# Last sublayer of a four-layer decoder: fp32 rows split into two float32r halves, and the last normalising moved to ScalarE

## Chip, cores and metric

The kernel runs on one core of a Trainium2 chip, as one launch. The metric is the device time of that launch in microseconds (us): before the change the median of three runs is 4253.46 us (4248.44 to 4256.29). "PE" is the matmul engine (TensorE), "PEld" its weight loads, "DVE" is VectorE, "ACT" ScalarE, "POOL" GpSimd, and "SP" the engine whose queue issues the DMAs.

## Reference, cut to the last sublayer

A decoder of four layers (self-attention, cross-attention and a feed-forward part each, with a different form in every layer) runs over 64 x 64 tokens of 256 channels. Every sublayer ends in `x = layernorm(x + sublayer(x))`. The change touches the last sublayer alone, a feed-forward part with ternary weights ("bitlinear"):

```python
def absmax_quant(x):
    gamma = max(abs(x), axis=-1, keepdims=True)
    x_hat = clip(x * 128 / gamma, -128 + EPS, 128 - EPS)
    return x_hat * gamma / 128                  # clipped, not rounded
def ternarize_weights(w):
    gamma = mean(abs(w))
    return sign(round(w / (gamma + EPS))) * gamma
def bitlinear(x, w):
    return einsum('bsd,od->bso', absmax_quant(layer_norm(x)), ternarize_weights(w))
h = gelu(bitlinear(x, w_fc), approximate=False) # w_fc: 1024 x 256
x = layernorm(x + bitlinear(h, w_proj))         # w_proj: 256 x 1024
```

All of it is fp32. The weights are -1, 0 or 1 times one number, and that number is applied after the product.

## The kernel before

**Tiles.** The 4096 tokens are 8 groups (`g`) of 4 tiles (`t`) of 128 tokens, 32 tiles in all. The rows `X[g]` stay in SBUF for the whole kernel, as do the eight buffers `CT[g]` (128 x 1024 fp32), which hold the transposed context until the cross-attention of layer 3 has read its group. After that the last sublayer uses `CT[g]` for the normalised and clipped rows of group `g` (`l3_prepare`).

**The last sublayer** (`l3_ffn`) walks over the 32 tiles with a pipeline that is written out for PE. In iteration `i`, PE has, in this order: the eight 128 x 128 transposes of tile `i-3` (`turned`, into two PSUM banks), the first product of tile `i` (`hidden`, 256 to 1024), in two of four tiles the transposes of the next group's rows (`turn`), and the second product of tile `i-3` (`output`, 1024 to 256). Around PE a tile needs, in this order:

- ACT: Gelu of the first product out of PSUM in two halves (L2402);
- DVE: statistics of the 1024 values in two halves (L339), joined (L342), variance plus epsilon (L311); POOL: the power -1/2 (L313); DVE: minus mean times that (`nmr`, L2337); ACT: the normalising, 128 x 1024 (`hn`, L2342);
- DVE: largest absolute value (`am`, L2348), two small steps (L2349, L2350), and the clipping in two passes over 128 x 1024 (L2353, L2354);
- PE: transposes (L319); ACT: two copies 128 x 512 out of PSUM (L2412); PE: the second product (L2419);
- DVE: scale and residual (`z`, L2421), statistics (L339, L342, L311); POOL: power (L313); DVE: the last normalising into `X` (L2423); SP: the DMA of the result.

While the first six groups run, `parts` adds a quarter of the same preparation (`l3_prepare`, L2334 to L2354) of the group two further on to each tile.

**Who sets the order.** PE's order is the program's (`manual_schedule` for PE). On DVE, ACT, POOL and SP a planner puts the instructions into an order when the program is built, with its own costs and times; on the chip every engine then takes its instructions strictly in that order, and each waits for the semaphores of what it reads.

**Weights.** `ternary` loads a weight (1 MB) into a buffer of the ring, DVE sums its absolute values over 128 x 2048 (L2315), POOL sums over the partitions (L2316), and then POOL (L2325) and DVE (L2326) replace the weight by -1, 0, 1 in four pieces, with `CT[3]` and `CT[4]` for scratch. The loads were issued at 3174.3 and 3199.4 us of the profiled execution, and the pieces made between 3520.8 and 3625 us, all inside the cross-attention before.

**fp32 on PE.** One `matmul` of fp32 operands in the program shows in the trace as two MATMUL records, each with a weight load of its own: the 4 products of `hidden` are 8 records, the 8 of `output` 16.

Of the kernel before, what the change touches and what calls it, by code (L numbers as in the profile page):

```python
# [9 lines left out]

F32 = mybir.dt.float32
BF16 = mybir.dt.bfloat16
# [19 lines left out]
class Linear:  # L32
# [68 lines left out]
    def first(self, pool, bank, fill):  # L101
# [41 lines left out]
class ContextRows:  # L143
# [3 lines left out]
    def __init__(self, dec):  # L147
# [12 lines left out]
    def fill(self, n, pool, tag, bufs, banks, copy):  # L160

        dec = self.dec
        while n and self.units:
# [12 lines left out]
class L1Ffn:  # L176
# [21 lines left out]
    def weights(self):  # L198
# [80 lines left out]
class Decoder:  # L279
# [2025 lines left out]
            late=late, ready=ready, key_turned=key_turned, turned=turned, scores=scores, output=output, values=values, end=end,  # L2305
        )

    def ternary(self, name):

        nc, ins = self.nc, self.ins  # L2310
        w = self.weight(name)
        n = ins[name].shape[1]
        self.load(w.rearrange("p (c n) -> p c n", n=n), ins[name].rearrange("(c p) n -> p c n", p=P))
        col, gam = self.small(1, "tcol", bufs=2), self.small(1, "tgam", bufs=2)
        nc.vector.tensor_reduce(col, w, AX.X, ALU.add, apply_absolute_value=True)  # L2315
        nc.gpsimd.partition_all_reduce(gam, col, P, bass_isa.ReduceOp.add)  # L2316
        nc.vector.tensor_scalar_mul(gam, gam, 1.0 / (P * WCOLS))

        thr = self.small(2, "tthr", bufs=2)
        nc.vector.tensor_scalar(thr[:, 0:1], gam, 1e-6, 0.5, ALU.add, ALU.mult)  # L2320
        nc.vector.tensor_scalar_mul(thr[:, 1:2], thr[:, 0:1], -1.0)
        for i in range(4):
            part = w[:, i * 512 : (i + 1) * 512]
            below = self.CT[3 + i // 2][:, i % 2, :]
            nc.gpsimd.tensor_scalar(below, part, thr[:, 1:2], None, ALU.is_lt)  # L2325
            nc.vector.scalar_tensor_tensor(part, part, thr[:, 0:1], below, ALU.is_gt, ALU.subtract)  # L2326
        return w.rearrange("p (c n) -> p c n", n=n), gam

    def l3_quantized(self, out, src, n):

# [42 lines left out]
    def l3_ffn(self, ctx):  # L2373

        nc = self.nc
        HID = 1024
        wfc, gfc = self.ternary("l3f_wfc")  # L2380
        wpr, gpr = self.ternary("l3f_wproj")
        AHEAD = 2
        wk = self.pool(ctx, "l3f", 2)
        groups, state = {}, {}

        def turn(g, c):
            if c == 0:
                groups[g] = wk.tile([P, 2, NTOK], F32, tag="xt", name="xt")
            ps = self.transpose4([self.l3_rows[g][:, t, c * P : (c + 1) * P] for t in range(TG)], "xt")
            nc.scalar.copy(groups[g][:, c, :], ps)  # L2390

        def hidden(g, t):
            xt = groups[g]
# [12 lines left out]
            return hn  # L2406

        def turned(h):
            ht = wk.tile([P, 8, P], F32, tag="ht", name="ht")
# [3 lines left out]
            return ht  # L2413

        def output(g, t, ht):
            x = self.X[g]
            ps = self.bank("o", tag="acc", bufs=2)
            for j in range(8):
                nc.tensor.matmul(ps[:, :D], ht[:, j, :], wpr[:, j, :], start=j == 0, stop=j == 7)  # L2419
            z = wk.tile([P, 1, D], F32, tag="z", name="z")  # L2420
            nc.vector.scalar_tensor_tensor(z[:, 0, :], ps[:, :D], gpr, x[:, t, :], ALU.mult, ALU.add)  # L2421
            mv, rstd = self.mean_rstd(z, 1, 1e-5)
            nc.vector.tensor_scalar(x[:, t, :], z[:, 0, :], mv[:, 0, 0:1], rstd, ALU.subtract, ALU.mult)  # L2423

        tiles = [(g, t) for g in range(self.n_groups) for t in range(TG)]
        n = len(tiles)
        with self.tc.manual_schedule(engines={mybir.EngineType.PE}):
            for g in range(len(self.l3_rows), AHEAD):
                for part in self.l3_prepare(g):
                    part()  # L2430
            groups[0] = self.l3_first
            parts, hts = [], {}
            for i in range(n + 3):

                for j in range(i - 3, i - 2 if i < n else min(i - 1, n)):
# [12 lines left out]
                if parts:  # L2448
                    parts.pop(0)()
# [93 lines left out]
```

## Time and profile before

| | |
|---|---|
| runs, median | 4253.46 us |
| span of the profiled execution | 4250.0 us |
| cross-attention of layer 3 ends (last product L2274) | 3963.8 us |
| last sublayer, from there to the end | 286 us |
| first products of the last sublayer, L2398 | 256 records of 128 x 512, 3963.4 to 4222 us |
| second products, L2419 | 512 records of 128 x 256 |
| Gelu, L2402 | 64 of 128 x 512, mean 689 ns |
| copies out of PSUM, L2412 | 64 of 128 x 512, mean 577 ns |
| last normalising, L2423 | 32 of 128 x 256 on DVE, mean 411 ns |
| power -1/2, L313 in the last sublayer | 65 of 128 x 1, mean 627 ns; 6 of 128 x 4, mean 1103 ns |

Busy time is the time in which an engine has an instruction in it; matmuls overlap one another, so the distance from one start to the next tells their cost better than the mean duration. The share of a whole span mixes stages with different limits; for the change only the last 286 us and the stage just before count.

### The profile page before, as it was taken

The page shows a single profiled execution, that of the slowest core. Times are in us where ns is not written, and L with a number is a line of the kernel's source. Part 1 is how long each engine was busy: PE and PEld are TensorE (multiplying, and loading weights), DVE is VectorE, ACT ScalarE, POOL GpSimd, SP SyncE. Part 2 cuts the span into 40 slices and gives each one's busy share as a digit, 9 for nine tenths or more (in the row PEclk, how much of TensorE's full clock was granted, in tenths as well). Part 3 has the DMA queues.
Part 4 walks back from the last instruction along what each step waited for, and adds up shares of the span by engine and source line. Part 5 has one row for each costly group of instructions (what it writes and reads, how often), then busy time and mean ns, then how long its engine had stood idle before and what let it go on. Part 6 is the DMA issues. An engine that isn't in the chain of part 4 may idle for free.

```text
span 4250.0 us, 74130 instructions
## 1 busy us (share of the span) xinstructions
PE 4051.5 (95%) x28788; PEld 2618.4 (62%) x28808; DVE 3042.7 (72%) x6107; ACT 2106.4 (50%) x3863; POOL 1506.3 (35%) x1553
## 2 busy tenths in 40 slices
PE   8889999989998999989999999999999999999998
PEld 5645556666675555546666666666656666666666
DVE  6844548888685688877777777777766777777786
ACT  5555635767634577544444444444433444444443
POOL 4511112242341111115555555555544444444111
PEclk9989999999999999999999999999999999999999
DMA  2200002333300000031111111111131100000000
GB/s 81 73 21 10 1 26 69 72 84 71 82 1 12 1 1 1 10 132 28 26 31 26 26 31 26 26 30 27 26 102 28 26 23 21 23 23 16 11 16 18
DMA packets 108294, 144.00 MB, mean 34 GB/s; under 512 B 15844, under 2 KB 73380, under 8 KB 106536
## 3 DMA queue, kind: packets, MB, share of 16 engines
q1 hardware_dynamic: 106984, 137.69, 12.7%
q8 instruction: 228, 3.74, 0.4%
q10 hardware_dynamic: 960, 1.57, 0.2%
q14 instruction: 122, 1.00, 0.1%
HBM read 70.25 MB, written 26.76 MB: 23 GB/s over the span
## 4 chain that ended last, share of the span: by engine, by line
PE 65%; DVE 15%; ACT 6%; POOL 4%; issue 3%; DMA 1%; SPq 0%; POOLq 0%; ACTq 0%; DVEq 0%
PE p L1777 19%; PE acc L2066 5%; PE acc L2274 4%; PE sq L1208 3%; PE ret L1247 2%; PE qT L319 2%; PE acc L1396 2%; POOL rstd L313 2%; DVE bnst L339 2%; PE gate L911 2%; DVE mc L1213 2%; PE gate L1592 2%; PE sk L1211 2%; PE s L2004 2%; PE up L911 2%
## 5 line engine op out<-in xcount | busy, mean ns | idle before, releaser
L313 POOL TENSOR_TENSOR rstd<-rstd,neg_half 128x1 f32<-128x1 f32 (+1 forms) x195 | 157.9, 810 | 653.1 <-DVE rstd L311 585.2
L313 POOL TENSOR_TENSOR hrq<-hrq,neg_half 128x4 f32<-128x4 f32 x256 | 258.7, 1011 | 300.7 <-DVE hrq L311 283.9
L1213 DVE TENSOR_REDUCE mc<-sq 128x2 f32<-128x512 f32 x512 | 317.1, 682 | 63.9 <-PE sk L1211 63.7
L1219 ACT ACTIVATE e<-sk 128x512 f32<-128x512 f32 x512 | 265.5, 608 | 112.1 <-PE sk L1211 111.5
L1208 PE MATMUL sq<-l1x 32*128 32x256 f32 x2048 | 275.2, 407 | 4.9 <-DVE z L1094 3.1
L1777 PE MATMUL p<-l3a_wq,xt 128*128 128x512 f32 x512 | 243.8, 599 | 11.2 <-DVE v L300 9.9
L313 POOL TENSOR_TENSOR hrk<-hrk,neg_half 128x4 f32<-128x4 f32 x160 | 188.2, 1176 | 185.8 <-DVE hrk L311 181.0
L1211 PE MATMUL sk<-l1x 32*128 32x256 f32 x2048 | 252.9, 392 | 0.0
L1777 PE MATMUL p<-l3a_wk,xt 128*128 128x512 f32 x512 | 247.1, 605 | 0.0
L1208 PEld LDWEIGHTS sq<-l1x 32*128 32x128 f32 x2048 | 208.3, 195 | 58.8 <-issue 23.6
L1777 PE MATMUL p<-l3x_wq,xt 128*128 128x512 f32 x512 | 242.3, 596 | 0.3 <-DVE k L2168 0.3
L1777 PE MATMUL p<-l3a_wv,xt 128*128 128x512 f32 x512 | 233.9, 599 | 0.4 <-ACT y L94 0.4
L2274 PE MATMUL acc<-l3x_wo,yt 128*128 128x256 f32 x1024 | 232.4, 380 | 1.6 <-DVE yt L300 1.0
L2066 PE MATMUL acc<-l3a_wproj,yt 128*128 128x256 f32 x1024 | 232.0, 379 | 0.5 <-DVE yt L300 0.5
L2066 PEld LDWEIGHTS acc<-l3a_wproj,yt 128*128 128x128 f32 x1024 | 194.2, 190 | 53.7 <-issue 29.2
L2274 PEld LDWEIGHTS acc<-l3x_wo,yt 128*128 128x128 f32 x1024 | 190.5, 190 | 33.9 <-issue 7.7
L1211 PEld LDWEIGHTS sk<-l1x 32*128 32x128 f32 x2048 | 188.5, 187 | 7.3 <-issue 2.9
L2237 POOL TENSOR_TENSOR s<-s,smx 128x512 f32<-128x512 f32 x64 | 66.9, 1046 | 333.8 <-DVE smx L2236 319.8
L319 PEld LDWEIGHTS qT<-ident,q 128*128 128x128 f32 x1024 | 121.9, 141 | 95.9 <-issue 75.2
L2050 POOL TENSOR_TENSOR hry<-hry,neg_half 128x8 f32<-128x8 f32 x64 | 106.2, 1659 | 183.4 <-DVE hry L2046 183.4
L319 PE MATMUL qT<-ident,q 128*128 128x128 f32 x1024 | 157.4, 277 | 3.3 <-ACT qT L2208 2.4
L1247 PE MATMUL ret<-e,vt 128*32 128x256 f32 x2048 | 140.6, 390 | 18.2 <-DVE mc L1213 17.2
(415 smaller groups left out, 10209.4 us busy)
## 6 DMA issues: line engine op xcount, KB each, us to landing
vs<-v SPq DMA_DIRECT2D x308, 128.0 KB
l3x_kv<-kv SPq DMA_DIRECT2D x28, 256.0 KB
x<-in_x SPq DMA_DIRECT2D x8, 512.0 KB
ct<-in_ctxT SPq DMA_DIRECT2D x8, 512.0 KB
cn<-in_ctx SPq DMA_DIRECT2D x8, 512.0 KB
l1x<-in_ctx SPq DMA_DIRECT2D x128, 32.0 KB
l1x_x<-x SPq DMA_DIRECT2D x8, 512.0 KB
l1x<-l1x_x SPq DMA_DIRECT2D x128, 32.0 KB
```

Of the source, the lines that this page charges most:

```text
L313: nc.gpsimd.tensor_tensor(out, out, self.neg_half[:, :n], ALU.pow)
L319: self.nc.tensor.transpose(ps[:, j * P : (j + 1) * P], blk, self.ident)
L911: nc.tensor.matmul(ps[:n], w[:, c, h0 : h0 + n], xt[:, c, :], start=c == 0, stop=c == 1)
L1208: nc.tensor.matmul(ps[:, n, :], x_[rows, j, part], c_[rows, j, :], start=True, stop=True)
L1211: nc.tensor.matmul(ps[:, n, :], c_[rows, j, part], x_[rows, j, :], start=True, stop=True)
L1213: nc.vector.tensor_reduce(mc[new % 2][:, ra + k, 2 * j : 2 * j + 2], ps, AX.X, ALU.max, negate=True)
L1219: nc.scalar.activation(es[rb + k], ps, AF.Exp, scale=scale)
L1247: nc.tensor.matmul(ret[32 * r : 32 * r + 32, :], vt[i % 2][:, lc, 4 * r + j, :], es[r][:, lc, :], start=lc == 0, stop=lc == 1,)
L1777: self.nc.tensor.matmul(ps, lhs(c), w(c, cols), start=c == 0, stop=c == 1 and bias is None)
L2050: nc.gpsimd.tensor_tensor(r, r, self.neg_half[:, :8], ALU.pow)
L2066: nc.tensor.matmul(acc[:, :D], yts[h % 2][:, h // 2, :], wp[n // 8][:, (n % 8) * D : (n % 8 + 1) * D], start=n == 0, stop=n == 15,)
L2274: nc.tensor.matmul(acc[:, :D], yts[h % 2][:, h // 2, :], w.o[n // 8][:, (n % 8) * D : (n % 8 + 1) * D], start=n == 0, stop=n == 15,)
```

## The change

Three things change.

1. **Two halves.** The rows that enter the two products are split. ACT copies the transposed values out of PSUM twice: once into a tile of type float32r (the value rounded to 12 bits of mantissa, `xhi`, `hhi`) and once as fp32 (`xt`, `ht`). POOL subtracts the one from the other into a second float32r tile (`xlo`, `hlo`), which holds the rest exactly. Each product becomes two float32r matmuls with the same weights, which are float32r as well: `hidden` has 8 instead of 4, `output` 16 instead of 8.
2. **Weights.** `ternary` loads the raw weight in two 512 KB pieces into `CT[3]` and `CT[4]` (for `l3f_wfc`) and `CT[5]` and `CT[6]` (for `l3f_wproj`), sums each piece on DVE, adds the sums, and writes -1, 0, 1 as float32r into the ring, with `CT[2]` for scratch. The loads can only be issued when the cross-attention has read those buffers for the last time.
3. **Last normalising.** The DVE pass over 128 x 256 (L2423) becomes a small DVE step (`nmr`) and an ACT pass.

The tile of the Gelu's result, `h`, has 2 buffers instead of 4.

```diff
-    def ternary(self, name):
+    def ternary(self, name, raw, spare):
...
-        self.load(w.rearrange("p (c n) -> p c n", n=n), ins[name].rearrange("(c p) n -> p c n", p=P))
-        nc.vector.tensor_reduce(col, w, AX.X, ALU.add, apply_absolute_value=True)
+        half = ins[name].rearrange("(h c p) n -> h p c n", h=2, p=P)
+        for i in range(2):
+            flat = raw[i].rearrange("p c n -> p (c n)")
+            self.load(flat.rearrange("p (c n) -> p c n", n=n), half[i])
+            nc.vector.tensor_reduce(col[:, i : i + 1], flat, AX.X, ALU.add, apply_absolute_value=True)
+        nc.vector.tensor_tensor(col[:, 0:1], col[:, 0:1], col[:, 1:2], ALU.add)
...
+        w = self.weight(name, F32R)
         for i in range(4):
-            part = w[:, i * 512 : (i + 1) * 512]
-            below = self.CT[3 + i // 2][:, i % 2, :]
+            part, below = raw[i // 2][:, i % 2, :], spare[:, i % 2, :]
...
+    def halves(self, src, hi, lo):
+        self.nc.gpsimd.tensor_tensor(lo, src, hi.bitcast(F32), ALU.subtract)
...
-        wfc, gfc = self.ternary("l3f_wfc")
-        wpr, gpr = self.ternary("l3f_wproj")
+        wfc, gfc = self.ternary("l3f_wfc", self.CT[3:5], self.CT[2])
+        wpr, gpr = self.ternary("l3f_wproj", self.CT[5:7], self.CT[2])
...
+        def split(g, c, src):
+            if c == 0:
+                groups[g] = [wk.tile([P, 2, NTOK], F32R, tag=n, name=n) for n in ("xhi", "xlo")]
+            hi, lo = (x[:, c, :] for x in groups[g])
+            nc.scalar.copy(hi, src)
+            return hi, lo
...
         def turn(g, c):
             ps = self.transpose4([self.l3_rows[g][:, t, c * P : (c + 1) * P] for t in range(TG)], "xt")
-            nc.scalar.copy(groups[g][:, c, :], ps)
+            hi, lo = split(g, c, ps)
+            xt = wk.tile([P, NTOK], F32, tag="xt", name="xt")
+            nc.scalar.copy(xt, ps)
+            self.halves(xt, hi, lo)
...
-            h = wk.tile([P, 1, HID], F32, tag="h", name="h", bufs=4)
+            h = wk.tile([P, 1, HID], F32, tag="h", name="h", bufs=2)
...
-                    nc.tensor.matmul(
-                        ps, xt[:, c, t * P : (t + 1) * P], wfc[:, c, i * 512 : (i + 1) * 512],
-                        start=c == 0, stop=c == 1,
-                    )
+                    for k, x in enumerate(groups[g]):
+                        nc.tensor.matmul(
+                            ps, x[:, c, t * P : (t + 1) * P], wfc[:, c, i * 512 : (i + 1) * 512],
+                            start=c == 0 and k == 0, stop=c == 1 and k == 1,
+                        )
...
-                nc.scalar.copy(ht[:, 4 * i : 4 * i + 4, :].rearrange("p j t -> p (j t)"), ps)
+                hi, lo = (x[:, 4 * i : 4 * i + 4, :].rearrange("p j t -> p (j t)") for x in hts)
+                nc.scalar.copy(hi, ps)
+                ht = wk.tile([P, NTOK], F32, tag="ht", name="ht")
+                nc.scalar.copy(ht, ps)
+                self.halves(ht, hi, lo)
...
-                nc.tensor.matmul(ps[:, :D], ht[:, j, :], wpr[:, j, :], start=j == 0, stop=j == 7)
+                for k in range(2):
+                    nc.tensor.matmul(
+                        ps[:, :D], ht[k][:, j, :], wpr[:, j, :], start=j == 0 and k == 0, stop=j == 7 and k == 1
+                    )
...
-            nc.vector.tensor_scalar(x[:, t, :], z[:, 0, :], mv[:, 0, 0:1], rstd, ALU.subtract, ALU.mult)
+            nb = self.small(1, "nmr", bufs=4)
+            nc.vector.scalar_tensor_tensor(nb, mv[:, 0, 0:1], -1.0, rstd, ALU.mult, ALU.mult)
+            nc.scalar.activation(x[:, t, :], z[:, 0, :], AF.Identity, bias=nb, scale=rstd)
...
-            groups[0] = self.l3_first
+            for c in range(2):
+                hi, lo = split(0, c, self.l3_first[:, c, :])
+                self.halves(self.l3_first[:, c, :], hi, lo)
```

The line numbers of the changed kernel are higher: what was L311, L313, L339, L2342, L2353 is L312, L314, L340, L2352, L2363 there, and the new steps are L2337 (subtraction of the halves), L2401 and L2408 (copies in `turn`), L2432 and L2434 (copies in `turned`), L2450 and L2451 (last normalising).

More of the change, by code (lines that the diff above doesn't have):

```diff
@@ L11 @@
 F32 = mybir.dt.float32
+F32R = mybir.dt.float32r
 BF16 = mybir.dt.bfloat16
@@ L2306, in l3_xattn @@
         )
-    def ternary(self, name):
+    def ternary(self, name, raw, spare):
         nc, ins = self.nc, self.ins
-        w = self.weight(name)
         n = ins[name].shape[1]
-        self.load(w.rearrange("p (c n) -> p c n", n=n), ins[name].rearrange("(c p) n -> p c n", p=P))
-        col, gam = self.small(1, "tcol", bufs=2), self.small(1, "tgam", bufs=2)
-        nc.vector.tensor_reduce(col, w, AX.X, ALU.add, apply_absolute_value=True)
-        nc.gpsimd.partition_all_reduce(gam, col, P, bass_isa.ReduceOp.add)
+        col, gam = self.small(2, "tcol", bufs=2), self.small(1, "tgam", bufs=2)
+        half = ins[name].rearrange("(h c p) n -> h p c n", h=2, p=P)
[4 more added lines that the diff above has]
+        nc.vector.tensor_tensor(col[:, 0:1], col[:, 0:1], col[:, 1:2], ALU.add)
+        nc.gpsimd.partition_all_reduce(gam, col[:, 0:1], P, bass_isa.ReduceOp.add)
         nc.vector.tensor_scalar_mul(gam, gam, 1.0 / (P * WCOLS))
@@ L2321, in ternary @@
         nc.vector.tensor_scalar_mul(thr[:, 1:2], thr[:, 0:1], -1.0)
+        w = self.weight(name, F32R)
         for i in range(4):
-            part = w[:, i * 512 : (i + 1) * 512]
-            below = self.CT[3 + i // 2][:, i % 2, :]
+            part, below = raw[i // 2][:, i % 2, :], spare[:, i % 2, :]
             nc.gpsimd.tensor_scalar(below, part, thr[:, 1:2], None, ALU.is_lt)
-            nc.vector.scalar_tensor_tensor(part, part, thr[:, 0:1], below, ALU.is_gt, ALU.subtract)
+            nc.vector.scalar_tensor_tensor(
+                w[:, i * 512 : (i + 1) * 512], part, thr[:, 0:1], below, ALU.is_gt, ALU.subtract
+            )
         return w.rearrange("p (c n) -> p c n", n=n), gam
+    def halves(self, src, hi, lo):
+        self.nc.gpsimd.tensor_tensor(lo, src, hi.bitcast(F32), ALU.subtract)
     def l3_quantized(self, out, src, n):
@@ L2384, in l3_ffn @@
         groups, state = {}, {}
+        def split(g, c, src):
[4 more added lines that the diff above has]
+            return hi, lo
         def turn(g, c):
-            if c == 0:
-                groups[g] = wk.tile([P, 2, NTOK], F32, tag="xt", name="xt")
             ps = self.transpose4([self.l3_rows[g][:, t, c * P : (c + 1) * P] for t in range(TG)], "xt")
-            nc.scalar.copy(groups[g][:, c, :], ps)
+            hi, lo = split(g, c, ps)
+            xt = wk.tile([P, NTOK], F32, tag="xt", name="xt")
+            nc.scalar.copy(xt, ps)
+            self.halves(xt, hi, lo)
         def hidden(g, t):
-            xt = groups[g]
-            h = wk.tile([P, 1, HID], F32, tag="h", name="h", bufs=4)
+            h = wk.tile([P, 1, HID], F32, tag="h", name="h", bufs=2)
             for i in range(2):
@@ L2408, in turned @@
         def turned(h):
-            ht = wk.tile([P, 8, P], F32, tag="ht", name="ht")
+            hts = [wk.tile([P, 8, P], F32R, tag=n, name=n) for n in ("hhi", "hlo")]
             for i in range(2):
                 ps = self.transpose4([h[:, 0, (4 * i + j) * P : (4 * i + j + 1) * P] for j in range(4)], "ht")
-                nc.scalar.copy(ht[:, 4 * i : 4 * i + 4, :].rearrange("p j t -> p (j t)"), ps)
-            return ht
+                hi, lo = (x[:, 4 * i : 4 * i + 4, :].rearrange("p j t -> p (j t)") for x in hts)
[3 more added lines that the diff above has]
+                self.halves(ht, hi, lo)
+            return hts
         def output(g, t, ht):
@@ L2418, in output @@
             for j in range(8):
-                nc.tensor.matmul(ps[:, :D], ht[:, j, :], wpr[:, j, :], start=j == 0, stop=j == 7)
+                for k in range(2):
+                    nc.tensor.matmul(
+                        ps[:, :D], ht[k][:, j, :], wpr[:, j, :], start=j == 0 and k == 0, stop=j == 7 and k == 1
+                    )
             z = wk.tile([P, 1, D], F32, tag="z", name="z")
```

## The prediction

> **What bounds the kernel now.** I read the page first, then the stages, then the last stage's chain of waits and its list of waits, and last the rows that price the new work.
>
> ```profile
> PE 4051.5 (95%) x28788; PEld 2618.4 (62%) x28808; DVE 3042.7 (72%) x6107; ACT 2106.4 (50%) x3863; POOL 1506.3 (35%) x1553
> ```
>
> By the page PE bounds the kernel, and a change that halves PE's passes should pay. The stage says less. This row is the last sublayer: start and end, length, then PE, PEld, DVE, ACT and POOL busy, granted clock, DMA share, GB/s.
>
> ```profile
> 3963.00:4250.00 287.00, 262.30 (x1084) 179.06 (x1082) 217.78 (x611) 130.94 (x200) 47.35 (x71) 0.98 0.05 15
> ```
>
> PE has work for 91% of the 287 us, DVE for 76%. The chain of waits over one of the last tiles (start, length, what) shows who sets the pace:
>
> ```profile
> 4203.91 1.25 ACT hn L2342
> 4205.18 1.22 DVE am L2348
> ...
> 4208.32 0.99 POOL rstd L313
> 4209.33 0.41 DVE x L2423
> 4209.74 1.20 DVE bnst L339 x2
> ...
> 4211.51 0.55 POOL rstd L313
> 4212.09 0.17 DVE nmr L2337
> 4212.34 1.25 ACT hn L2342
> ```
>
> From `hn` to the next `hn` are 8.43 us, and PE isn't in it. DVE, with short trips to POOL and ACT, closes the loop; PE, which needs 0.87 (eight transposes) + 3.44 (eight records at 0.43) + 3.46 (sixteen at 0.216) = 7.77 us a tile, is 0.66 us short of being the limit. What DVE waited for in the stage (total, times, longest):
>
> ```profile
> DVE am L2348 <- ACT hn L2342: 22.7, 18, 1.4
> DVE nmr L2337 <- POOL rstd L313: 19.6, 32, 0.7
> ...
> DVE x L2423 <- POOL rstd L313: 10.5, 22, 0.7
> ...
> DVE z L2421 <- PE o L2419: 5.4, 4, 2.1
> ```
>
> The first three make 52.8 us: DVE sits before a step whose input POOL or ACT is making from DVE's own last result. Only 5.4 us are waits for PE's products. With 7.1 us of single waits at the start (3.7 + 2.7 + 0.7) the list is 65.3 us, and 217.8 busy + 65.3 waiting + 3.9 at both ends = 287. So the sum is made on DVE's account, not on PE's.
>
> **PE, removed.** No float32r operation is in the trace. Its price lies between two rows: bf16 (one pass: 128x512 records 0.216 us apart) and fp32 (0.43 apart). At the low end the eight matmuls of `hidden` cost 1.73 us. For `output` the pass over 256 columns would be 0.11 us, and the load of 128 fp32 weight columns has a floor that shows where the moving side is only 16 columns wide:
>
> ```profile
> 1300.69 0.59 PE L1378 MATMUL gate<-xt,l_signs 128*128 128x512 bf16 x2
> ...
> 9.42 1.85 PE L704 MATMUL v<-l0a,xt 128*128 128x16 f32 x16
> ```
>
> Two bf16 matmuls take 0.59 with 0.38 for one, so 0.21 apart; sixteen loads 1.85, so 0.11 apart: no more than the pass. `output` is then 16 x 0.11 = 1.8 us, and a tile 4.4 us in place of 7.77: 3.4 us x 32 = 108 us less PE work. At the high end (0.43 and 0.216 apart) the new matmuls, as many as the old records, cost what the old did and PE gains nothing. I take the low end: the change halves the mantissa that each pass has to carry, which is nearer to bf16's case than to fp32's. Little of the 108 us is on the path, as the chain showed. What it does free is PE as a second limit 0.66 us behind the first.
>
> **DVE.** Removed: 32 x 0.411 (L2423) = 13.2 us; added: 32 small `nmr` at 0.159 (L2337's row) = 5.1 us. Busy 217.8 - 8.1 = 209.7.
>
> **DVE's waits.** The planner lays the queue out anew. In the order of both built programs I added the durations of the DVE instructions that stand between each `rstd` (L311) and the step that needs its power, against the 0.72 us that the trip to POOL takes in the chain above, and between `nmr` and `am` against 1.5 us for ACT's 1.24 and its two handovers (1.2 for the 128x4 power). For the old order what is missing adds up to 50 us (52.8 measured); for the new one to 20 us (5 before `nmr`, 7 before the last normalising's step, 6 before `am`, 2 for the prepared rows). Tile and next tile are now interleaved: a typical stretch has 0.9 to 2.5 us of other work in front of `am`, where the old one had none. That is the gain: 33 us off the measured waits. The other 12.5 us I leave.
>
> **ACT, added.** 64 copies x 0.577 (`ht`), 14 x 0.586 in `turn`, two from SBUF at the start, 32 x 0.596 for the last normalising (L2342's 128x256 row) = 65 us on 131: 196 of some 274. Hidden behind DVE's 210 and its waits; each 0.1 us a tile by which ACT came to lag would cost 3.2 us. SP's 32 result DMAs stay as many and now wait for ACT's 0.60 in place of DVE's 0.41: 0.2 us once, at the end. The loop through PE, Tr 0.44, four copies 2.3, POOL's half 1.27, last eight matmuls 0.9, is 4.9 us a tile, under 8. `h` with two buffers makes Gelu `i` wait for `hn` of `i-2`, two periods earlier: nothing, unless `hn` comes a whole period late.
>
> **POOL, added.** 64 + 16 subtractions 128x512, both inputs whole: nearest row is 1.27 us (L2161, bias added to 128x512 on POOL; rows with a broadcast input are 1.04). 80 x 1.27 = 102 us on 47. POOL's time is free, but two things aren't: the power stands behind a half in POOL's queue, and DVE and POOL get in each other's way.
>
> ```profile
> L2013 DVE TENSOR_TENSOR s<-s,mxx x64: 679/694/1306, 1907.3 to 3151.8; 128x512 f32<-128x512 f32 x64
> ...
> L311 DVE TENSOR_SCALAR hrk<-hrk x87: 157/169/1247, 2601.3 to 3923.9; 128x4 f32<-128x4 f32 x87
> ```
>
> In the attention stages, where POOL is busy half the time, the maximum of the same DVE instruction (last of min/median/max, ns) is 0.6 to 1.1 us over its median; the long ones begin while POOL has a 128x512 pass running. The mean excess there is 0.10 us (all 416 `hrq` and `hrk` steps: 265 to 272 ns against 170). With five small steps and two clipping passes a tile at 0.10 that is 0.7 us, x 32 = 22 us; bounds: none, as now (L2353 never above 0.755), and 0.38 (share of the halves in the stage, 102/270) x half a half-pass 0.64 x 7 = 1.7 us a tile, 55 us. For the power behind a half: none to 2 x 0.38 x 0.64 = 0.5 us a tile; 0.15 taken, since 0.2 to 0.8 us of other DVE work usually covers it: 5 us.
>
> The Trainium skill speaks against the change here: "SBUF — State Buffer", section "SBUF: two separate sides", has DVE and GpSimd share a port pair under an exclusive lock held for the whole instruction, the other fully blocked, for GpSimd passes against DVE's two-port modes and two-input operations. The two rows agree that whole passes are waited out. Taken literally, with random meetings, the sum goes to the upper bound, 33 us more, and the time to about 4274; the means of the rows say that the meetings are rarer, so I keep 0.10.
>
> **Weights.** Four 512 KB loads enter SP's queue between the loads of `vs` for groups 3 to 6 and wait there for PE's last reading of `CT`; behind them stand `vs` pieces needed a step (about 12 us) later. The 1 MB load issued at 3174.3 had been landed and read from 3179.2 on, so 512 KB is 2.5 us: covered by the step; 10 us if not. DVE's sums are 4 x 1.21 for 2 x 2.28; POOL's pieces the same. That stage is PE's (767 us busy of the 783 from 3180 to 3963): nothing. At the start, copy 0.58, half 1.27 twice before the first Gelu, but ACT's table load (1.28) stands there now: 0.5 us.
>
> **Sum.** 209.7 + 20 + 12.5 + 0.5 + 22 + 5 + 3.9 = 273.6 against 287: -13.4 us. The profiled execution's 4250 lies 3.5 us under the median of the runs, so I carry the difference over: 4253.5 - 13.4 = 4240.
>
> **Rivals.**
> *No contention* (15%): POOL's halves fall into DVE's free moments, as the planner arranged: 27 us less, 4213; with the order's missing 20 us halved by it, 4203. For it: L2353 unhurt today. Against: today POOL holds nothing longer than 1 us here.
> *PE doesn't get faster* (12%): float32r at fp32's distance; PE 7.77 + 0.19 (turns) a tile, 255 us, plus fill and some of DVE's stalls, 275 to 290 us: 4242 to 4257, about no change. Against it the bf16 row. Four times the one-pass price, 4500 us, has no row and gets 2% of it.
> *POOL's halves take more than the order gives* (23%, the slower side): the place is POOL's queue in each tile, where powers wait behind halves and DVE's port steps wait behind both, and ACT's `hn`, copies and Gelus wait behind `nmr`. The gain ahead of contention is 287 - 247 = 40 us, so it decides from 1.25 us a tile on. At 2.0 us a tile (the upper bounds 1.7 + 0.5, a little cut) it costs 64 us: 4277. For it: the maxima above, and an ACT that isn't idle any more.
> *The forecast* has 50%, with a range of its own of 4225 to 4255.
>
> **The numbers.** About 0.2% (8.5 us) is what a measurement of this kernel can tell from no change. Faster by more, under 4245: the no-contention case, two thirds of the forecast and some of PE's, 0.52. Within: 0.23. Slower, over 4262: 0.25. The range is 4207 to 4272.
>
> **What will show it.** Right: in the last stage PE under 170 us busy with matmuls 0.216 and 0.11 apart, DVE about 210 busy and the chain still DVE's; waits of `am` for `hn` under 10 us. Contention: durations of L312 and L2363 above 0.3 and 0.9, powers that last over 1 us. Wrong: matmuls 0.43 apart; an ACT busy for over 230 us; a cross-attention that ends later than 3968.

## The result and the profile after

| | median us | runs | ratio to before (95% interval) |
|---|---|---|---|
| before, runs beside it | 4252.16 | 4248.44 to 4256.29 | |
| changed | 4271.29 | 4267.11 to 4274.29 | 1.0045 (1.0030 to 1.0059) |

The change made the kernel 19 us slower; 4240 had been predicted. The profiled execution of the changed kernel took 4267.11 us, its span is 4265.4 (before: 4250.0). First the engines' busy time on the page of the changed kernel:

```profile
PE 3990.9 (94%) x28788; PEld 2612.3 (61%) x28808; DVE 3062.6 (72%) x6111; ACT 2163.7 (51%) x3975; POOL 1611.5 (38%) x1633
```

PE did lose 61 us of work, and the time rose all the same. The stages tell where. The cut lies here at the cross-attention's last `output` product (L2274, L2275 after), and the cross-attention is counted from its first one. Columns: start and end, length, then PE, PEld, DVE, ACT, POOL busy, granted clock, DMA share, GB/s. Before:

```profile
3206.90:3963.80 756.90, 746.67 (x5555) 516.92 (x5554) 563.26 (x1106) 311.54 (x550) 316.99 (x315) 1.00 0.09 21
3963.80:4250.00 286.20, 261.50 (x1080) 178.34 (x1078) 217.78 (x611) 130.94 (x200) 47.35 (x71) 0.98 0.05 15
```

After:

```profile
3201.50:3972.30 770.80, 747.43 (x5554) 518.94 (x5552) 562.68 (x1112) 310.45 (x549) 317.37 (x316) 0.99 0.09 24
3972.30:4265.40 293.10, 202.35 (x1080) 170.56 (x1080) 240.33 (x611) 188.90 (x312) 151.27 (x151) 0.83 0.05 15
```

The cross-attention, whose own computation the change leaves alone, takes 13.9 us longer; the last sublayer takes 6.9 us longer. The stage starts 5.4 us earlier here, which is mostly scatter: over all the kernels below it starts at 3201.5 to 3211.4 with the new ternary step and at 3206.5 to 3211.6 with the old one. 13.9 + 6.9 - 5.4 = 15.4, the difference of the spans.

In the last sublayer PE is busy for 69% and the clock granted to it is 0.83; DVE has 22.6 us more work than before, where the forecast had 14 (8 less, and 22 for contention). What DVE waited for there (total, times, longest):

```profile
DVE nmr L2347 <- POOL rstd L314: 25.4, 28, 2.9
DVE nmr L2450 <- POOL rstd L314: 9.4, 20, 1.3
DVE bnst L340 <- ACT h L2421: 6.5, 2, 5.5
DVE z L361 <- PE acc L2275: 3.7, 1, 3.7
DVE am L2358 <- ACT hn L2352: 2.1, 4, 0.8
```

The wait of `am` for `hn`, 22.7 us before, is down to 2.1: the new order does what was read out of it. Waits for the power stayed, 34.8 us against 30.1. Two stretches of the timeline, DVE's instructions first, then POOL's, show what is new (start, length, instruction, idle time before it and its releaser):

```profile
4193.97 0.47 DVE L2447 SCALAR_TENSOR_TENSOR z<-o,tgam,x 128x256 f32<-128x256 f32 x1
4194.77 1.22 DVE L2347 SCALAR_TENSOR_TENSOR nmr<-bnmv,rstd 128x1 f32<-128x1 f32 x1 [0.34 <-POOL rstd L314]
...
4201.60 1.68 DVE L2364 TENSOR_SCALAR hn<-hn,am 128x1024 f32<-128x1024 f32 x1
```

```profile
4194.19 0.55 POOL L314 TENSOR_TENSOR rstd<-rstd,neg_half 128x1 f32<-128x1 f32 x1 [3.66 <-DVE rstd L312]
4194.71 1.27 POOL L2337 TENSOR_TENSOR hlo<-ht,hhi 128x512 fp32r<-128x512 f32 x1
...
4201.45 1.28 POOL L2337 TENSOR_TENSOR xlo<-xt,xhi 128x512 fp32r<-128x512 f32 x1
```

`nmr` works on one number per partition and takes 0.16 us. It waits for the power; POOL ends the power and at once begins the half queued behind it; `nmr` begins 0.06 us into that half and ends as the half ends, 1.22 us later. The clip at 4201.60, which begins 0.15 us into a half, takes 1.68 us in place of 0.74. In the whole sublayer 12 of the 32 `nmr` of L2450 and 9 of the 38 of L2347 begin while a half runs: those take 1.10 and 1.08 us on average, the others 0.157 and 0.159. Each of these 21 ends 0.01 to 0.02 us after the half, and 15 of them begin within 0.08 us of its start. Of the 64 clips over 128x1024, 30 begin in a half, 28 of them over 0.1 us into it; they take 1.31 us on average and end 0.55 us or more after the half, the others take 0.73.

In the cross-attention two steps stand out (a step is counted from its first `output` product to that of the next): 23.1 and 20.7 us where the same steps took 11.9. DVE's row, then POOL's, in the first of them:

```profile
3624.06 0.17 DVE L312 TENSOR_SCALAR hrq<-hrq 128x4 f32<-128x4 f32 x1
3632.70 1.19 DVE L2330 SCALAR_TENSOR_TENSOR l3f_wfc<-ct,tthr,ct 128x512 fp32r<-128x512 f32 x1 [8.47 <-POOL ct L2329]
```

```profile
3615.81 0.40 POOL L2320 PARTITION_ALL_REDUCE tgam<-tcol  x1 [6.08 <-DVE s L2230]
3623.84 1.05 POOL L314 TENSOR_TENSOR hrq<-hrq,neg_half 128x4 f32<-128x4 f32 x1 [7.62 <-ACT sq L2145]
...
3630.07 1.01 POOL L314 TENSOR_TENSOR hrq<-hrq,neg_half 128x4 f32<-128x4 f32 x1
3631.09 6.21 POOL L2329 TENSOR_SCALAR ct<-ct,tthr 128x512 f32<-128x512 f32 x4
```

DVE's ternary piece stands in DVE's queue ahead of the next step's attention work and waits 8.47 us for a comparison that POOL has behind seven other instructions of its own. Afterwards PE waits 9.5 us for a copy of ACT's (`xt`, L2288), which stands in ACT's queue behind `sq` (L2145), and `sq` waits for DVE's `q`.

What makes POOL late is, by the traces, the all-reduce, with which `ternary` sums over the partitions (L2320): POOL is idle for 6.08 us before it and for 7.62 us behind it. In the kernel before, the second weight's all-reduce (L2316) stood in the first step of the cross-attention:

```profile
3207.65 0.42 POOL L2316 PARTITION_ALL_REDUCE tgam<-tcol  x1 [5.84 <-DVE tcol L2315]
3215.09 1.03 POOL L2237 TENSOR_TENSOR s<-s,smx 128x512 f32<-128x512 f32 x1 [7.01 <-DVE mxx L2232]
```

Here POOL's second row begins 5.2 us after its input was there (DVE's reciprocal `smx`, L2236, ended at 3209.84). That first step took 20.4 us; in the changed kernel, without an all-reduce in it, it takes 14.1. So the stage adds up: 21.3 us more in the two long steps and the two right behind them, 6.3 less in the first, 1.1 less elsewhere, 13.9 in all. The traces of all the kernels below agree: wherever `ternary` has an all-reduce, POOL is idle for 5.7 us or more before it and for 6.7 to 7.6 behind it, and the step of this stage in which the second idle time ends is long. No run takes the all-reduce alone out of a step, so its share is read and not tested.

### The profile page after: what moved, and what is told of

The parts are those of the page before. It is cut to its first block, busy times and chain, and to the rows that moved or that the text cites. A ratio compares the mean times of both kernels' runs of the same rounds, so it can differ in the third digit from the quotient of the medians.

```text
span 4265.4 us, 74387 instructions
## 1 busy us (share of the span) xinstructions
PE 3990.9 (94%) x28788; PEld 2612.3 (61%) x28808; DVE 3062.6 (72%) x6111; ACT 2163.7 (51%) x3975; POOL 1611.5 (38%) x1633
## 5 line engine op out<-in xcount | busy, mean ns | idle before, releaser
L314 POOL TENSOR_TENSOR hrq<-hrq,neg_half 128x4 f32<-128x4 f32 x256 | 258.2, 1009 | 319.7 <-DVE hrq L312 297.5
L314 POOL TENSOR_TENSOR rstd<-rstd,neg_half 128x1 f32<-128x1 f32 (+1 forms) x195 | 157.8, 811 | 472.7 <-DVE rstd L312 442.1
L314 POOL TENSOR_TENSOR hrk<-hrk,neg_half 128x4 f32<-128x4 f32 x160 | 188.4, 1177 | 184.6 <-DVE hrk L312 179.9
L1778 PE MATMUL p<-l3a_wq,xt 128*128 128x512 f32 x512 | 243.8, 599 | 11.2 <-DVE v L301 9.9
L2275 PE MATMUL acc<-l3x_wo,yt 128*128 128x256 f32 x1024 | 233.5, 381 | 0.6 <-ACT yt L299 0.3
L2275 PEld LDWEIGHTS acc<-l3x_wo,yt 128*128 128x128 f32 x1024 | 191.9, 191 | 32.8 <-issue 7.7
```

Of the source, the lines that this page charges most:

```text
L314: nc.gpsimd.tensor_tensor(out, out, self.neg_half[:, :n], ALU.pow)
L1778: self.nc.tensor.matmul(ps, lhs(c), w(c, cols), start=c == 0, stop=c == 1 and bias is None)
L2275: nc.tensor.matmul(acc[:, :D], yts[h % 2][:, h // 2, :], w.o[n // 8][:, (n % 8) * D : (n % 8 + 1) * D], start=n == 0, stop=n == 15,)
```

## The experiments

Times are medians; "stage" is the last sublayer and "attention" the cross-attention of the profiled execution, cut as above (before 286.2 and 756.9 us, changed 293.1 and 770.8).

| kernel | median us | before beside it | ratio (95% interval) | stage | attention |
|---|---|---|---|---|---|
| b_tern | 4266.7 | 4253.9 | 1.0030 (1.0019 to 1.0041) | 288.1 | 770.6 |
| a_old_tern | 4259.8 | 4253.9 | 1.0014 (1.0005 to 1.0023) | 292.2 | 758.2 |
| b_dummy | 4265.1 | 4253.9 | 1.0027 (1.0015 to 1.0038) | 298.0 | 757.4 |
| a_hi_only | 4203.0 | 4253.9 | 0.9880 (0.9867 to 0.9894) | 226.4 | 770.6 |
| a_hi_twice | 4214.3 | 4253.5 | 0.9912 (0.9897 to 0.9927) | 236.8 | 771.6 |
| a_hi_pool | 4267.1 | 4253.5 | 1.0031 (1.0019 to 1.0042) | 289.1 | 771.0 |
| a_spare4 | 4275.7 | 4253.5 | 1.0051 (1.0036 to 1.0066) | 292.2 | 775.1 |
| a_pe_lo | 4341.8 | 4253.5 | 1.0205 (1.0190 to 1.0221) | 359.4 | 774.7 |
| b_norm | 4262.1 | 4253.9 | 1.0019 (1.0010 to 1.0029) | 296.4 | 757.5 |
| a_tern_dve | 4260.0 | 4253.9 | 1.0018 (1.0008 to 1.0028) | 295.1 | 760.3 |
| a_hi_copy | 4213.4 | 4253.9 | 0.9914 (0.9898 to 0.9931) | 238.6 | 770.5 |
| a_fc_only | 4217.0 | 4253.9 | 0.9917 (0.9902 to 0.9931) | 249.6 | 762.8 |
| a_norm_dve | 4269.3 | 4252.6 | 1.0038 (1.0026 to 1.0050) | 289.1 | 770.7 |
| a_fc_norm_dve | 4218.1 | 4252.6 | 0.9916 (0.9894 to 0.9937) | 254.5 | 759.9 |

### The ternary step

**b_tern**: `before` with the changed `ternary` and its two calls, `w` staying fp32.

> The kernel before, with the change's ternary step alone: the raw weights loaded in halves into CT[3:5] and CT[5:7], one scratch CT[2] of two slots, the result written into a weight tile (fp32 here). The last sublayer stays as it was. Theory T (the ternary step holds up the cross-attention): its last output product ends some 8 us later than 3963, with two steps of 20 us and more where 12 is usual, and the kernel takes 4252 + 8 = 4260. Rival L (the loss is made in the last sublayer alone, whatever the stage before loses being made good in its first tiles): 4252, ratio 1.000.

Attention 770.6 us, steps of 22.2 and 20.9 us in the same two places, the time 12.8 us up. The step alone makes the cross-attention's whole loss; nothing of it is made good later.

**a_old_tern**:

```
-        wfc, gfc = self.ternary("l3f_wfc", self.CT[3:5], self.CT[2])
+        wfc, gfc = self.ternary("l3f_wfc")
...
+        w = self.weight(name + "_raw")
...
+        wr = self.weight(name, F32R)
```

> The changed kernel with the old way of the ternary step: raw weights loaded whole into a weight tile early, four scratch slots in CT[3:5], the result written as float32r into a second weight tile. The last sublayer stays as changed. Theory T: the two long steps of the cross-attention go, it ends at 3963 or up to 6 us earlier, and the time falls by 8 to 14 us from the changed kernel's 4271 to 4257 to 4263, still not below the kernel before: the rest is the last sublayer's. Rival L: 4271 stays.

Attention 758.2 us, longest step in the old places 17.8 (in it ends the idle time behind this kernel's second all-reduce, at 3627.1; the other long step is back at 11.9); 11.5 us off the changed kernel's time, as theory T had it. With the old step the changed kernel would still be behind the one before.

**a_spare4**: `below = spare[i // 2][:, i % 2, :]` with `self.CT[1:3]` for `self.CT[2]`. `CT[1]` holds the prepared rows of group 1 by then, so those rows are lost in the result, and pieces 3 and 4 had to wait until they had been made.

> The changed kernel with four scratch slots (CT[1:3]) in place of two (CT[2]) for the ternary step; the loads in halves stay. Theory T1 (the two long steps of the cross-attention come from the two slots: POOL's third piece waits for DVE's first one): they go, the cross-attention ends near 3960 and the time is about 4260. Rival T2 (they come from the loads and the sums of absolute values, which now stand in the queues one step ahead of the pieces): the two steps stay over 20 us, and 4271.

That spoils the kernel as a version but makes the test sharper. Only two of the first weight's pieces stand in the long step now, and it is still 21.6 us long (DVE, then POOL):

```profile
3626.67 0.17 DVE L312 TENSOR_SCALAR hrq<-hrq 128x4 f32<-128x4 f32 x1
3634.78 1.19 DVE L2330 SCALAR_TENSOR_TENSOR l3f_wfc<-ct,tthr,ct 128x512 fp32r<-128x512 f32 x1 [7.94 <-POOL ct L2329]
```

```profile
3633.18 3.12 POOL L2329 TENSOR_SCALAR ct<-ct,tthr 128x512 f32<-128x512 f32 x2
```

So it isn't the number of scratch slots: T1 falls. The second long step, 20.7 us, has no ternary piece of DVE's in it at all. There DVE waits for a power that POOL has behind an all-reduce (3821.6), seven instructions and two comparisons:

```profile
3840.44 0.16 DVE L367 SCALAR_TENSOR_TENSOR nmr<-bnmv,rstd 128x1 f32<-128x1 f32 x1 [7.16 <-POOL rstd L314]
```

**a_tern_dve**: `nc.vector.tensor_scalar(below, ...)` for `nc.gpsimd.tensor_scalar(below, ...)`.

> The changed kernel with the ternary step's eight comparisons on DVE in place of POOL; loads, scratch and the last sublayer stay. Theory T3 (each long step of the cross-attention is DVE standing in its queue for a comparison that POOL reaches only after its other work of that step): the two steps of 20 us and more are back at 12 to 15, the cross-attention ends near 3955 to 3962 and the kernel takes 4257 to 4262. Rival T2 (the loads and sums do it): the long steps stay, 4271.

The two steps are 16.9 and 15.4 us, the time is 11.3 us under the changed kernel's. With the steps right behind them they are 11.0 us longer than before, not 21.3: DVE's wait for POOL's late comparisons was about half of the loss. Loads, sums and both all-reduces (3624.8 and 3822.4) are placed as in the changed kernel, and the other half stayed, so T2 falls only in part.

### The halves

**a_hi_only**: the calls of `halves`, the copies to `xt` and `ht`, and the second pass are taken out.

> The changed kernel with the upper halves alone: no lower halves, so no subtraction on POOL, no second copy on ACT, and one pass in place of two; the products lack the lower 12 bits of the rows. Theory P: the last sublayer falls to DVE's 210 us of work and the 32 us of waits that the sum of the prediction left, 240 to 255 us in place of 293, the time to 4222 to 4238, although PE idles more and its granted clock stays low. Rival C (the clock and the waits for PE set the pace): the clock falls below 0.84, and the time stays over 4255.

Even less than theory P said: 226.4 us, at a clock of 0.78. A low clock and an idle PE don't by themselves make the stage slow. PE's second pass is gone here too; a_hi_twice below puts it back. Now the 67 us between 226 and 293 in pieces.

**a_hi_copy**: as a_hi_only, but with `nc.scalar.copy(xt, ps)` and `nc.scalar.copy(ht, ps)`.

> As a_hi_only (one pass, products without the lower halves), with ACT's second copies made as in the changed kernel and read by nobody, and without POOL's subtractions. Only POOL tells this kernel from a_hi_pool, whose last sublayer took 289 us, and only the copies tell it from a_hi_only with 226. Theory P: 226 to 235 us. Rival A (ACT's 45 us more are late for DVE): 250 us or more.

**a_hi_pool**: as a_hi_copy, with `self.halves(xt, hi, lo)` and `self.halves(ht, hi, lo)` as well, their result unread.

> As a_hi_only, but ACT's second copies and POOL's subtractions are made as in the changed kernel, and nobody reads what they leave: one pass, products without the lower halves. Theory P (POOL's presence costs, not the wait for its result): DVE again over 230 us busy, waits for the power over 25 us, the last sublayer 275 to 293 us. Rival D (what costs is that PE waits for the lower halves, 28 us in the changed kernel, and the tile is late by that): 226 to 245.

The last sublayers of a_hi_only, a_hi_copy and a_hi_pool, one line of each kernel's windows:

```profile
3976.00:4202.40 226.40, 131.53 (x697) 114.78 (x696) 196.23 (x611) 153.48 (x234) 53.19 (x71) 0.78 0.06 19
```

```profile
3973.10:4211.70 238.60, 144.76 (x696) 121.83 (x696) 196.86 (x611) 186.54 (x312) 50.91 (x71) 0.77 0.05 18
```

```profile
3978.70:4267.80 289.10, 156.15 (x696) 131.53 (x696) 244.12 (x611) 187.97 (x312) 156.42 (x151) 0.71 0.05 15
```

The copies cost 12.2 us, and DVE's busy time (third of the five) doesn't move: they turn into DVE's waits. But with them the planner also laid DVE's queue anew (99 of its 611 instructions keep their place), so the 12.2 may be in part the order's. From a_hi_copy to a_hi_pool DVE's order stays (597 of 611 keep their place). POOL's subtractions, which nobody reads, cost 50.5 us, and 47.3 of that is DVE busier with the same 611 instructions. Rival D falls. Which instructions, from the groups of a_hi_copy and then of a_hi_pool (busy us, mean ns, idle before):

```profile
L2358 DVE TENSOR_REDUCE am<-hn 128x1 f32<-128x1024 f32 x32 | 38.6, 1206 | 1.3 <-ACT hn L2352 1.3
L2364 DVE TENSOR_SCALAR hn<-hn,am 128x1024 f32<-128x1024 f32 x32 | 23.6, 739 | 0.0
L2448 DVE SCALAR_TENSOR_TENSOR nmr<-bnmv,rstd 128x1 f32<-128x1 f32 x32 | 5.1, 159 | 12.3 <-POOL rstd L314 11.4
```

```profile
L2358 DVE TENSOR_REDUCE am<-hn 128x1 f32<-128x1024 f32 x32 | 38.5, 1204 | 1.2 <-ACT hn L2352 1.2
L2364 DVE TENSOR_SCALAR hn<-hn,am 128x1024 f32<-128x1024 f32 x32 | 35.3, 1103 | 0.0
L2450 DVE SCALAR_TENSOR_TENSOR nmr<-bnmv,rstd 128x1 f32<-128x1 f32 x32 | 22.2, 695 | 18.8 <-POOL rstd L314 18.1
```

The reduction doesn't feel POOL; the clip and the step after the power do. By the groups' busy time the `nmr` make 26 of the 47 us, the clips 18.

**a_hi_twice**: as a_hi_only with two passes, both over `xhi` and `hhi`.

> As a_hi_only, but every product takes two passes, both over the upper half: PE has the changed kernel's work, POOL none of its subtractions and ACT not the second copy; the products come out as twice those of the upper halves. The last sublayer took 226 us with one pass and 293 with both halves. Theory P (the 67 us between are POOL's): 226 to 235. Rival C (PE's second pass, on a lower clock, has a good part in them): 250 or more.

236.8 us in the profiled execution, 11.3 us more than a_hi_only by the medians: PE's second pass isn't free once nothing else is in the way, but it is no 67 us (and here too the order changed with it). With PE's whole work back and a clock of 0.88 the stage stays under rival C's 250, though a little over theory P's 235. Beside POOL's halves it and the wait for them add 4.0 us (289.1 to 293.1).

**b_dummy**: `before`, and after the copy of `ht` in `turned`:

```
+                src = ht[:, 4 * i : 4 * i + 4, :].rearrange("p j t -> p (j t)")
+                nc.gpsimd.tensor_tensor(wk.tile([P, NTOK], F32, tag="lo", name="lo"), src, src, ALU.subtract)
```

> The kernel before, with two subtractions 128x512 a tile added on POOL (64 in all) whose results nobody reads; they leave PE, ACT and every dependence of the result as they were. Theory P (POOL's passes cost by the port that DVE and POOL share and by the power queued behind them): DVE's steps after the power and its clipping passes grow as in the changed kernel (0.3 to 0.5 us in place of 0.16, 0.98 in place of 0.74), the last sublayer takes 20 to 40 us longer, 4272 to 4292. Rival C (POOL's passes are harmless by themselves; the changed kernel loses by PE's waits and its lower clock): within 5 us of 4252.

Between the two: 11.2 us. The stage is 11.8 us longer, DVE 15.4 us busier, its waits about as before. These passes with one input twice take 1.06 us and not 1.35, and the planner had laid the queues otherwise: 6 of the 38 `nmr` of L2337 began within one, where in a_hi_pool 9 of the 38 of L2347 did and 16 of the 32 of L2450, a step that this kernel doesn't have. What a pass on POOL costs hangs on whom it meets.

### The order, and the last normalising

**b_norm**: `before` with the last three lines of the changed `output`.

> The kernel before, with the last normalising alone moved to ScalarE (and a small DVE step for its bias). DVE has 8 us less. Theory N (DVE sets the pace and the planner's new order carries the gain, as the prediction had it): the waits of DVE fall with the new order, and the last sublayer goes from 286 us to what PE with its 7.8 us a tile allows, 255 to 270; 4222 to 4237. Rival M (the new order came with float32r, not with this step): 278 to 286 us, 4245 to 4253.

Rival M, and worse: 8.2 us slower than the kernel before. DVE's first waits there:

```profile
DVE nmr L2337 <- POOL rstd L313: 25.7, 36, 1.0
DVE am L2348 <- ACT hn L2342: 25.4, 23, 1.4
DVE nmr L2424 <- POOL rstd L313: 9.9, 22, 0.7
```

DVE is 6 us less busy, but its order is no better than before's; all its waits sum up to 81 us against 65.

**a_norm_dve** and **a_fc_norm_dve** (the reverse edit in the changed kernel and in a_fc_only).

> The changed kernel with the last normalising back on DVE. Theory O (the order comes with the shorter float32r products; the last normalising on ScalarE is worth its 8 us of DVE work and the port that its small step waits for): DVE's waits for hn stay under 5 us, the last sublayer takes 288 to 300 us, the time 4266 to 4280. Rival N (the last normalising on ScalarE brings the order): waits for hn over 15 us and a last sublayer over 305 us. Rival H (it hurts, as it did in the kernel before): under 286 us, 4264 and less.

> a_fc_only with the last normalising back on DVE: float32r for the first product alone, no subtractions on POOL but none either of the last normalising's steps on ScalarE. Theory O: DVE 8 us busier, 218 us, waits as in a_fc_only; the last sublayer 252 to 262 us in place of 250, the time 4219 to 4230. Rival N: over 270 us, 4240 and more. Rival H: under 247 us, 4214 and less.

Waits for `hn` of 0.9 and 1.4 us: the good order doesn't come with the last normalising. It goes with shorter products, but every kernel that has it also has `h` with two buffers, and no run separates the two; a_pe_lo, below, has the two buffers, long products and the poor order, so the buffers alone don't bring it. The last normalising on ScalarE is worth nothing that can be told: 2.0 us slower with it in the changed kernel, 1.1 faster in the other, both inside the intervals.

### Two versions

**a_pe_lo**: the lower half made on PE, and a_spare4's scratch, with the same rows lost.

```
+                    nc.tensor.matmul(ps[:, part], blk, self.ident, start=True, stop=False)
+                    nc.tensor.matmul(ps[:, part], neg, hi[:, part], start=False, stop=True)
+                nc.scalar.copy(lo, ps)
```

> A version meant to beat both: four scratch slots, and the lower halves made without POOL. When ACT has copied the upper half, PE writes the turned block again by fp32 products with the identity and adds the upper half times minus the identity in float32r (16 small matmuls a tile more); ACT copies the lower half from there. ACT has as many copies as in the changed kernel, POOL none of the subtractions but the first two. Theory P: DVE is back at about 197 us busy and PE at some 5.8 us a tile, the last sublayer takes 230 to 255 us and the kernel 4195 to 4222. Rival C (PE's work and waits on a low clock set the pace): the last sublayer stays over 275 us, 4240 and more.

A miss, beyond rival C's bound. A block's pair of products takes 0.34 us, not 0.17 (the fp32 product with the identity is two records). PE is busy for 294.6 of the 359.4 us, 9.2 us a tile and not 5.8, and DVE waits 40.0 us for `hn` again: the order is a poor one here.

**a_fc_only**: float32r for the first product alone, its lower half on DVE straight from PSUM; the second product fp32 as before; a_tern_dve's comparisons.

```
+            nc.vector.tensor_tensor(lo, ps, hi.bitcast(F32), ALU.subtract)
...
+        wpr, gpr = self.ternary("l3f_wproj", self.CT[5:7], self.CT[2], F32)
```

> A version meant to beat both: float32r halves for the first product alone, where a group of four tiles needs two subtractions and not ten; they run on DVE, from PSUM. The second product stays fp32 as before (one copy on ACT, no halves), the last normalising is on ScalarE, the ternary step's comparisons are on DVE. Theory P: nothing of the halves is on POOL, so DVE's steps keep their lengths: 197 + 16 x 0.69 = 208 us busy and 30 us of waits, PE 0.87 + 1.75 + 3.46 + 0.2 = 6.3 us a tile; the last sublayer takes 235 to 250 us, the kernel 4195 to 4215. Rival C (PE with its waits and a lower clock sets the pace): over 265 us, 4225 and more.

It beats both kernels: 4217.0 us, 36.9 under the one before. Its last sublayer:

```profile
3971.00:4220.60 249.60, 217.78 (x1080) 184.56 (x1080) 209.56 (x627) 152.25 (x234) 47.26 (x71) 0.95 0.05 18
```

DVE is 209.6 us busy, as expected, and PE, with 217.8, a little more than DVE. The stage lies within the range expected, the time 2 us over it; the attention takes 5.9 us more than before.

## Why the prediction was wrong

**PE, removed: right.** The low end was the right one. With PE warm, float32r products of 512 columns are 0.23 us apart, of 256 columns 0.12:

```profile
4191.28 0.28 PE L2443 MATMUL o<-l3f_wproj,hhi 128*128 128x256 f32 x1
4191.40 0.28 PE L2443 MATMUL o<-l3f_wproj,hlo 128*128 128x256 f32 x1
...
4193.16 0.39 PE L2417 MATMUL h<-l3f_wfc,xlo 128*128 128x512 f32 x1
4193.39 0.39 PE L2417 MATMUL h<-l3f_wfc,xhi 128*128 128x512 f32 x1
```

Elsewhere (4205.6 to 4207.3) they are 0.43 apart. The granted clock, third from the end of each row, is 1.00 in the stretch of the last two products above and 0.50 there:

```profile
4192.80:4194.70 1.90, 1.90 (x11) 1.58 (x10) 1.64 (x7) 0.97 (x2) 0.51 (x1) 1.00 0.00 0
4205.60:4207.30 1.70, 1.70 (x5) 1.32 (x4) 1.28 (x7) 1.26 (x4) 1.41 (x2) 0.50 0.27 87
```

So PE is busy for 202.4 us in the stage and not for under 170, the sign that the prediction named; a_hi_only was the fastest at a clock lower still. That little of PE's saving lay on the path was right too.

**The order's gain: right for `am`, half right for the power.** `am` waits 2.1 us (6 forecast). The two `nmr` wait 34.8 us, against 14 forecast (5, 7, and 2 for the prepared rows). Without halves and second copies, in an order somewhat different (a_hi_only), they wait 17.1, near the forecast.

**POOL, added: the size that failed in the stage.** Contention was put at 0.10 us for each of seven steps a tile, 22 us in all. Set against a_hi_copy's means, the changed kernel's `nmr` (11.3 + 5.1 us, and 3.2 for the prepared rows'), clips (7.8 + 9.0 + 2.0) and 128x4 `am` (2.2) are 40.6 us longer: 1.27 us a tile against 0.7. The 0.10 was the mean of `hrq` and `hrk`, steps ahead of the power, over three stages. L2013, printed beside them, has a mean of 0.987 us against the median of 0.694, so 0.29 more. The five small steps don't suffer alike either: the step ahead of the power, L312 on 128x1, has 0.143 us here, and the prediction looked for contention there. The step after the power suffers, and 15 times in 21 by no chance meeting: the power's end releases it and the half behind the power at one moment. The `nmr` make 19.6 of the 40.6 us; the clips, 18.8, mostly meet a half that is already running and wait it out.

The power's own wait behind a half, 5 us in the sum, was at most 3: between a_hi_copy and a_hi_pool DVE's idle time grows from 41.7 to 45.0 us.

The Trainium skill, "SBUF — State Buffer", section "SBUF: two separate sides", taken literally gave 4274, beside 4271.3 measured; but of that gap to the forecast 14 us are the ternary step's, so it was near for another reason in part. Its section "Who interferes with whom" says that reductions don't contend with GpSimd, while instructions with two SBUF inputs and those in two-port modes do. The runs agree: the reduction takes 1.206 and 1.204 us without and with POOL's halves, the two-input `nmr` 0.159 and 0.695, a clip 0.739 and 1.103.

**ACT, added: "hidden" was wrong by some 12 us.** From a_hi_only to a_hi_copy, which adds the copies alone to the program, it is 10.4 us by the medians. ACT isn't full (187 of 239 us), but of PE's waits before transposes 16.5 us, in seven pieces, now end with a copy of `xt` (L2408), and DVE's `z` waits for `o` 7.8 us and not 1.9. The two `nmr` wait 22.6 and not 17.1; they wait for POOL, so that part is rather the new order's. How the 12 us divide between copies and order isn't shown.

**DVE, removed: too small.** Without the port's share DVE is busy for 240.3 - 40.6 = 199.7 us, not 209.7. Rows of the trace overlap by up to 0.1 us when one instruction follows the other without a wait, so fewer waits also make the busy time less (33.0 us of overlap in the stage before, 39.6 in the changed kernel).

**Weights: "nothing" was wrong by 13.9 us, twice what the stage itself lost.** Not followed was the queue of the engines that make the pieces: "POOL's pieces the same" counts work, and its place had changed. The raw data are loaded at 3510 to 3809 in place of 3174 to 3200, so each weight's all-reduce and pieces come late. They fell into two of PE's steps, the all-reduce, around which POOL is idle for 13 us and more, then DVE's piece ahead of the attention's work and POOL's comparison behind it. The sum has no term for the all-reduce's new place. That stage being PE's is no cover for 8 us in which DVE does nothing, since PE needs DVE's work of each step. The prediction named the sign itself, a cross-attention that ends later than 3968; it ended at 3972.3.

**The start**: 3.5 us from the last `output` product to the first Gelu's product, where 0.5 was put for the start. The prediction counted from Gelu's table load, but PE's first product waits for `xhi`, and the second one for `xlo`.

**The sum.** The stage was forecast at 273.6 us and took 293.1: -10.0 (DVE's work), +18.6 (port), +10.9 (idle time: 52.8 in place of 41.9). The ternary step's 13.9 us came on top, less the 5.4 us by which the cross-attention began earlier.

**The rivals.** No contention and PE not faster are excluded. The third, POOL's halves taking more than the order gives, named the place nearly right: the price, 1.27 us a tile on DVE, is at the 1.25 from which it was to decide. It alone would have made about no change; the power's waits, the copies, the start and the ternary step made it a loss.

## What to carry to other kernels

Moving work to an engine that "has time" has to be priced at the instruction it will meet. Look for the step that a result of that engine releases: if the new work is queued behind that result, the meeting happens whenever the work is ready, and a step of 0.16 us pays a whole pass. Long passes like the clips pay as well, when they meet one by chance: nearly half of the price here. A mean over steps that stand elsewhere says little of either.

Preparing work hidden in a stage of another engine stays hidden only while no in-order queue puts a piece whose input is late, or an instruction that holds its engine long, ahead of that stage's own work; when its data are moved, read the order of all engines around each piece, not of the DMA queue alone, and the idle time around it as well as its own length. Where a change has several parts, the part that pays may be small: float32r for the first product alone, with its 16 subtractions on DVE and the comparisons off POOL, ended 36.9 us under the kernel before, the whole change 19 us above it.

## What the runs showed of the hardware

- Float32r products stood 0.23 us apart for 512 columns and 0.12 for 256 at a granted clock of 1.00, and 0.43 for 512 at 0.50.
- The clock granted in the last sublayer went from 0.98 (before, PE busy for 91% of it) over 0.83 (changed, 69%) to 0.71 (a_hi_pool, 54%), and the fastest stage of all (226.4 us) had 0.78.
- Under POOL's halves the DVE's `tensor_scalar` of 128x1 (0.143 and 0.138 us for L312 without and with them) was unhurt, that of 128x4 (`am`) went from 0.150 to 0.738, and the step that reads PSUM (`z`, 0.474 and 0.466) was unhurt too.
- Around each all-reduce over the partitions in `ternary`, itself 0.4 to 0.7 us long in the trace, POOL was idle for 5.7 us or more before and 6.7 to 7.6 us behind.
- A subtraction 128x512 with two inputs and a float32r result took 1.35 us on POOL, with one tensor as both inputs 1.06.
